# Sorting a 48-wide block for two pairs of graphs at once in a graph-network kernel

## The chip, the cores and the metric

The kernel runs on one core of a Trainium2 chip. The metric is the device time of one execution in microseconds (us), as the median of several runs. TensorE (PE) does the matrix products, VectorE (DVE) the elementwise work on whole tiles, ScalarE (ACT) activations and most copies out of PSUM, GpSimd (POOL) the indirect transfers, and SyncE (SP) starts most plain DMA transfers.

## The reference

There are 16 graphs of 1024 nodes with 64 channels, and a symmetric 0/1 adjacency of some 16 edges per node. Two layers follow one another, and each is added to its input.

```python
h = jnp.maximum(_layernorm(x, axis=-1), 0.0)
# layer 0: drop some edges of nodes with more than 10 neighbours, then
vals = jnp.where(nd[..., None], x[:, None, :, :], jnp.inf)   # nd: edges that are left
s = jnp.sort(vals, axis=2)                                   # over the neighbours
for tau, w in zip((0.25, 0.5, 0.75), (0.25, 0.5, 0.25)):     # weighted quantiles
    pos = tau * max(nv - 1, 0);  agg += w * (interpolation of s at pos)
y = relu((x + agg) @ W1 + b1) @ W2 + b2                      # times the mask
# layer 1: three graph convolutions relu(adj @ (x @ W) + b) with batch norm,
# their results side by side through one last weight, relu
```

For every node and channel, layer 0 needs three quantiles of the values of that node's live neighbours. That is where the kernel spends most of its time.

## The kernel before

**Pairs and blocks.** The graphs are handled in eight pairs, the 64 channels of two graphs on 128 partitions. In each pair the nodes are ordered by their number of live neighbours and get a place from 0 to 1023. Places with similar degrees form blocks (BLOCKS, line 39): seven blocks, 200, 192, 200, 176, 120, 72 and 48 places wide, with 11, 13, 15, 17, 19, 21 and 26 slots for neighbours, and last the tail (TAIL, line 44) of 16 places with 42 slots.

**Preparing a pair.** `prepare` (line 585) loads the adjacency rows in float32, makes an 8-bit copy `edgeT` of its transpose and stores it for later, clears the diagonal (line 686, a multiplication of 8 by 128 elements), works out which edges stay, ranks the nodes (the sign sums of line 770), scatters the rows to DRAM by place with indirect DMAs on POOL (line 778), reads them back (`lp`, line 794), transposes them, and numbers the neighbours of every place into `st.r` (line 851). At the end it rereads `h` (line 623) and splits it into three bfloat16 parts `hp`. It is a generator with 93 steps per pair.

**Gathering and sorting a block.** `gather` (line 959) builds, for several slots at a time, a one-hot tile `s` by an equality test on VectorE (line 987) and multiplies it with `hp` on TensorE (line 1018); ScalarE copies the sums to the block's tile `g` (line 1023). `sort_block` (line 1073) runs a sorting network on `g` and a spare tile `t`: each tuple of a network (NETS, line 77) is one VectorE instruction, a minimum or maximum of up to n1 by n2 rows of the block's width at once (line 935). Then the ranks that some quantile may need are multiplied by coefficients that ScalarE made (lines 868 and 871) and are added up (lines 941 and 950). The tiles `g` rotate over two buffers, `t` and `coef` have one.

**The tail** is too narrow to sort alone. In pairs 0 to 6 it is gathered into a buffer of another tag ("a", shared with the adjacency rows and the reread `h`) and sent to `tail_d` in DRAM; `sort_tails` (line 1090) reads several pairs' tails back side by side (line 1096) and sorts them together: pairs 0 to 3 at the start of pair 4, pairs 4 to 6 at the start of pair 7. The tail of pair 7 is sorted alone, at the end. POOL copies the tail's part of `st.z`, which the coefficients need, at the start of each pair's first gather (line 1065).

**Order of the work.** `weave` (line 1106) emits the network of one block instruction by instruction, and between these, by shares of the sort's cost, the gather of the next block and steps of the next pair's preparation. The shares come from SHARES (line 31): of the 93 steps, so many beside block 0, block 1 and so on, none beside block 6, where the first gather of the next pair stands. The framework's scheduler orders each engine's queue from there and keeps to this order by and large. In the last pair the second half of the computation, `later` (line 1228), takes the place of the preparation, with 7 steps beside each block (STEPS), but none beside `sort_tails`; after the last sort it goes on alone until the end.

```python
STEPS = 7
TAILS = {4: (0, 4), 7: (4, 7)}
weave(sort_block(st, n, pools), gather_block(st, n + 1, pools), steps)
```

## Time and profile before

| | |
|---|---|
| median of three runs | 3128.42 us (3122.96 to 3139.51) |
| the profiled execution: its own time | 3163.56 us |
| span from first to last instruction in it | 3161.8 us |
| PE, DVE, ACT, POOL busy | 2599.2, 2559.8, 1696.2, 619.5 us |
| mean granted TensorE clock | 0.915 |
| end of the last sort | 2832 us after the span's start |

The sum of a block's quantiles is written by the last addition of line 950, and the trace gives the start of each of these. Their distances are the stages of a pair. Of pair 2, which is one of the undisturbed ones in the middle, the seven blocks took 34.7, 40.3, 48.0, 46.5, 38.0, 46.2 and 46.8 us. In pair 7 the nine stages (block 0, tails of pairs 4 to 6, blocks 1 to 6, own tail) took 60.4, 50.5, 36.6, 78.2, 53.9, 45.6, 39.1, 39.2 and 48.7 us. What comes after the last sort takes 329.7 us.

A busy time is the time in which an engine had some instruction at work. Instructions overlap at their ends, so the mean duration of a kind of instruction, times their number, comes out above the busy time; distances between starts don't have this fault.

### The profile page before, as it was taken

The page shows a single profiled execution, that of the slowest core. Times are in us where ns is not written, and L with a number is a line of the kernel's source. Part 1 is how long each engine was busy: PE and PEld are TensorE (multiplying, and loading weights), DVE is VectorE, ACT ScalarE, POOL GpSimd, SP SyncE. Part 2 cuts the span into 40 slices and gives each one's busy share as a digit, 9 for nine tenths or more (in the row PEclk, how much of TensorE's full clock was granted, in tenths as well). Part 3 has the DMA queues.
Part 4 walks back from the last instruction along what each step waited for, and adds up shares of the span by engine and source line. Part 5 has one row for each costly group of instructions (what it writes and reads, how often), then busy time and mean ns, then how long its engine had stood idle before and what let it go on. Part 6 is the DMA issues. An engine that isn't in the chain of part 4 may idle for free.

```text
span 3161.8 us, 67201 instructions
## 1 busy us (share of the span) xinstructions
PE 2599.2 (82%) x27849; PEld 1697.4 (54%) x27849; DVE 2559.8 (81%) x5895; ACT 1696.2 (54%) x3292; POOL 619.5 (20%) x545
## 2 busy tenths in 40 slices
PE   2678978898888889885798889888986688977778
PEld 1445655565556556653565566456643456644445
DVE  4149889998999799989998999899976979963332
ACT  4764666567557755774367557745853223332221
POOL 5110161022102200330022103300422530311110
PEclk9779999999899999997899999999987799988989
DMA  4131022111211212122111211211113011122211
GB/s 138 46 104 60 3 67 70 56 55 52 66 57 54 64 56 68 46 72 47 42 64 51 66 56 57 67 56 63 48 36 75 9 41 26 49 55 54 54 54 42
DMA packets 221082, 177.45 MB, mean 56 GB/s; under 512 B 189024, under 2 KB 189152, under 8 KB 216672
## 3 DMA queue, kind: packets, MB, share of 16 engines
q1 hardware_dynamic: 141824, 125.88, 13.1%
q0 software_dynamic: 17408, 37.81, 3.9%
q10 hardware_dynamic: 61536, 9.39, 1.7%
q8 instruction: 219, 3.59, 0.5%
q14 instruction: 95, 0.78, 0.1%
HBM read 124.44 MB, written 48.55 MB: 55 GB/s over the span
## 4 chain that ended last, share of the span: by engine, by line
DVE 40%; PE 29%; ACT 12%; DMA 8%; issue 6%; another core or an unknown queue 2%; POOL 2%; ACTq 1%; DVEq 0%; POOLq 0%; SPq 0%
PE pg L1018 11%; DVE t L935 10%; DVE s L987 9%; DVE g L935 8%; PE pg L1200 5%; ACT junk L770 3%; DMA a<-in_adj 3%; DMA lp<-live_d 3%; DVE junk_v L673 2%; PE pr L845 2%; DVE g_tails L935 1%; DVE t_tails L935 1%; PE keys L763 1%; PE pf L1216 1%
## 5 line engine op out<-in xcount | busy, mean ns | idle before, releaser
L1018 PE MATMUL pg<-s,hp 128*64 128x400 bf16 (+11 forms) x16848 | 1366.5, 313 | 172.3 <-DVE s L987 138.1
L1018 PEld LDWEIGHTS <-hp 128*64 128x64 bf16 x16848 | 894.5, 112 | 553.9 <-issue 109.6
L987 DVE TENSOR_SCALAR s<-r 128x3200 bf16<-128x3200 bf16 (+25 forms) x1312 | 623.6, 521 | 103.6 <-PE pg L1018 74.9
L778 POOL DMA_INDIRECT live_d<-edge,place x128 | 261.1, 2040 | 1354.3 <-DVE place L773 1149.9
L1023 ACT COPY g<-pg 128x400 f32<-128x400 f32 (+10 forms) x384 | 169.0, 443 | 399.4 <-PE pg L1018 363.1
L935 DVE TENSOR_TENSOR t<-g 128x600 f32<-128x600 f32 (+9 forms) x524 | 315.5, 626 | 34.0 <-ACT g L1023 33.2
L1200 PE MATMUL pg<-adjT,xw 128*64 128x512 fp8e4 x2304 | 284.5, 398 | 52.8 <-ACT xw L1185 25.7
L935 DVE TENSOR_TENSOR g<-t 128x96 f32<-128x96 f32 (+16 forms) x555 | 283.2, 537 | 1.2
L1243 POOL DMA_INDIRECT agg<-agg_d,place x128 | 171.2, 1338 | 495.2 <-PE pt L1131 258.2
L671 ACT ACTIVATE edge<-a 128x1024 fp8e4<-128x1024 f32 x128 | 135.1, 1058 | 214.4 <-DMA a<-in_adj 213.9
L1200 PEld LDWEIGHTS <-xw 128*64 128x64 bf16 x2304 | 140.1, 114 | 182.4 <-issue 42.0
L868 ACT ACTIVATE coef<-z,bias 128x200 f32<-128x200 bf16 (+6 forms) x480 | 173.9, 405 | 102.3 <-DVE agg L950 66.0
L935 DVE TENSOR_TENSOR t<-t 128x192 f32<-128x192 f32 (+20 forms) x447 | 207.8, 475 | 0.2
L871 ACT ACTIVATE coef<-coef,wcol 128x200 f32<-128x200 f32 (+7 forms) x512 | 189.6, 403 | 9.3 <-issue 7.1
L673 DVE SCALAR_TENSOR_TENSOR junk_v<-a 128x1024 fp8e4<-128x1024 f32 x128 | 155.4, 1214 | 24.4 <-DMA a<-in_adj 24.4
L845 PE MATMUL pr<-liveT,upto 128*128 128x512 fp8e4 (+2 forms) x384 | 127.4, 350 | 53.1 <-ACT r L851 46.9
L770 ACT ACTIVATE junk<-keys,minus 128x1024 fp8e4<-128x1024 f32 x128 | 144.3, 1128 | 38.1 <-PE keys L763 34.3
L851 ACT CAST r<-pr 128x592 bf16<-128x592 f32 (+1 forms) x256 | 142.5, 585 | 41.1 <-PE pr L847 32.1
L794 POOL DMA_DIRECT2D lp<-live_d x128 | 89.4, 699 | 376.9 <-PE pt L809 319.3
L812 ACT ACTIVATE liveT<-pt 128x1024 fp8e4<-128x1024 f32 x128 | 130.3, 1034 | 50.5 <-PE pt L809 47.1
L752 ACT ACTIVATE edge<-q,bias 128x1024 fp8e4<-128x1024 f32 x128 | 141.8, 1108 | 22.6 <-PE q L747 22.6
L725 ACT ACTIVATE stays<-cs,back 128x1024 f16<-128x1024 f32 x128 | 136.7, 1111 | 31.1 <-PE cs L721 15.9
(182 smaller groups left out, 3879.4 us busy)
## 6 DMA issues: line engine op xcount, KB each, us to landing
a<-in_adj SPq DMA_DIRECT2D x128, 512.0 KB
adjT_d<-edgeT SPq DMA_DIRECT2D x16, 1024.0 KB
lp<-live_d POOLq DMA_DIRECT2D x128, 128.0 KB
adjT<-adjT_d SPq DMA_DIRECT2D x16, 1024.0 KB
room<-in_x SPq DMA_DIRECT2D x16, 256.0 KB
h_d<-room SPq DMA_DIRECT2D x16, 256.0 KB
h_again<-h_d SPq DMA_DIRECT2D x16, 256.0 KB
xt<-in_x SPq DMA_DIRECT2D x16, 256.0 KB
```

The source lines that it names most:

```text
L673: nc.vector.scalar_tensor_tensor(junk, a, 1.0, a, ALU.is_equal, ALU.not_equal, accum_out=odd[:, b, t : t + 1], saturate=False)
L770: nc.scalar.activation(junk, keys, AF.Sign, bias=minus[:, t : t + 1], accum_out=above[:, t : t + 1], saturate=False)
L778: sent = nc.gpsimd.indirect_dma_start(out=live_d[b][:, :], out_offset=bass.IndirectOffsetOnAxis(ap=place[:, b, t : t + 1], axis=0), in_=ed ...
L845: nc.tensor.matmul(out=pr[:, o], lhsT=upto, rhs=liveT[:, u, sl], start=True, stop=(u == 0))
L868: nc.scalar.activation(coef[:, i, :], z[:, at], AF.Abs, bias=bias(rank - (slots + 1) // 2 + tau), scale=sign)
L871: nc.scalar.activation(coef[:, i, :], coef[:, i, :], AF.Relu, bias=wcol[:, q : q + 1], scale=-w)
L935: nc.vector.tensor_tensor(view(bufs, o, n1, n2), view(bufs, a, n1, n2), view(bufs, b, n1, n2), ALU.max if op else ALU.min)
L987: nc.vector.tensor_scalar(s[:, k, :, us, w0:], r[:, :, us, at + w0 : at + W], float(LIVE + 1 + k0 + k), None, ALU.is_equal)
L1018: summed = nc.tensor.matmul(out=pg[x * C : (x + 1) * C, ks, w0:], lhsT=st.hp[:, part, x, u, :], rhs=s[:, ks, x, u, w0:], start=(whole and ...
L1023: nc.scalar.copy(g[:, k0 : k0 + n, :], pg)
L1200: nc.tensor.matmul(out=pg[cs, :], lhsT=part[:, u, cs], rhs=adjT[x][:, u, sl], start=(u == 0 and k == 0), stop=(u == NT - 1 and k == len(xw ...
L1243: nc.gpsimd.indirect_dma_start(out=agg[:, t, x, :], out_offset=None, in_=agg_d[b][:, :], in_offset=bass.IndirectOffsetOnAxis(ap=place[:, b ...
```

## The change

The block of 48 places (block 6, now named MID) is handled like the tails. In an even pair it is gathered and sent to `mid_d` in DRAM, and not sorted. In the odd pair after it, `rows_of_pairs` takes a buffer twice as wide, reads the even pair's rows back into its left half, and the odd pair's block is gathered straight into the right half; `sort_pairs` then sorts 96 places at once. An even pair has six sorting stages, an odd pair seven, and SHARES has a row for each.

In an even pair the block is gathered ahead of block 5, beside the sort of block 4, into the front of block 5's own buffer, from where it is stored; then block 5 is gathered into that buffer. The tail of an even pair is gathered in the last stage, beside the first gather of the next pair, instead of one stage ahead of that.

The tails of pairs 4 to 7 are sorted together: the tail of pair 7 is gathered first of its blocks, into the last columns of the tiles that are read back, and the tails' sort has 7 steps of `later` beside it. The parts of `st.z` for both sorts are copied by ScalarE (one copy for each pair and part) instead of POOL.

The networks of 13, 15, 19 and 26 slots are others. In instructions: 29 as before, 30 for 31, 57 for 60, and 85 for 95; the number of rows they compare is the same. The network of 13 needs 15 spare rows for 17. The multiplications by coefficients are one more for 19 and for 26 slots (the ranks stand otherwise).

The diagonal is cleared by a bitwise and of 8 by 32 words of 32 bits with a constant. Some scratch tiles are dropped or lie in others' room (the junk of the sign sums in `stays`, the junk of the bounds in PSUM, `h` of `later` in the older `hp` buffer, `step` in a pool of its own).

The diff, without the tables of the networks:

```diff
-SHARES = (10, 9, 17, 24, 20, 13, 0)
+SHARES = ((12, 12, 21, 27, 21, 0), (10, 9, 17, 24, 20, 13, 0))
 STEPS = 7
...
 
-TAILS = {4: (0, 4), 7: (4, 7)}
+TAILS = {4: (0, 4), 7: (4, 8)}
 TAIL = (1008, 1024, 21, 42)
+
+MID = len(BLOCKS) - 1
 
 
...
     nc.vector.tensor_copy(ident_16, ident)
+
+    off_diag = const.tile([P, P // 4], I32, name="off_diag")
+    nc.vector.tensor_scalar(off_diag[:, :].bitcast(U8), ident, -255.0, 255.0, ALU.mult, ALU.add)
     other_h = const.tile([P, P], BF16, name="other_h")
...
-    TW = TAIL[1] - TAIL[0]
-    tail_d = [dram.tile([P, TAIL[3], TW], F32, name=f"tail_d{p}") for p in range(NP)]
-
-    tail_z = const.tile([P, len(TAUS), NP, TW], BF16, name="tail_z")
+    MW, TW = (b[1] - b[0] for b in (BLOCKS[MID], TAIL))
+    part_d = {
+        MID: [dram.tile([P, BLOCKS[MID][3], MW], F32, name=f"mid_d{p}") for p in range(NP)],
+        MID + 1: [dram.tile([P, TAIL[3], TW], F32, name=f"tail_d{p}") for p in range(NP)],
+    }
+
+    part_z = {
+        MID: const.tile([P, len(TAUS), 2, MW], BF16, name="mid_z"),
+        MID + 1: const.tile([P, len(TAUS), 4, TW], BF16, name="tail_z"),
+    }
...
     def diagonal(e):
 
+        e = e[:, :, :].bitcast(I32)
         dims = [list(d) for d in e.ap]
-        return bass.AP(tensor=e.tensor, offset=e.offset, ap=[dims[0], [N + P, NT], [1, P]])
+        return bass.AP(tensor=e.tensor, offset=e.offset, ap=[dims[0], [(N + P) // 4, NT], [1, P // 4]])
...
         nc.sync.dma_start(out=adjT_d[b][:, :, :], in_=edgeT)
         own = diagonal(edgeT)
-        nc.vector.tensor_tensor(own, own, other_h[:, None, :].to_broadcast([P, NT, P]), ALU.mult, saturate=False)
+        nc.vector.tensor_tensor(own, own, off_diag[:, None, :].to_broadcast([P, NT, P // 4]), ALU.bitwise_and)
...
         above = work.tile([P, NT], F32, tag="above", name="above")
+
+        junk = stays[:, 0, : N // 2].bitcast(F8)
         for t in range(NT):
-            junk = work.tile([P, N], F8, tag="junk", name="junk")
             nc.scalar.activation(
                 junk, keys, AF.Sign, bias=minus[:, t : t + 1], accum_out=above[:, t : t + 1], saturate=False
             )
...
-            junk = work.tile([P, N], F8, tag="junk", name="junk")
             nc.scalar.activation(
-                junk[: 2 * NT, :], by, AF.Relu, accum_out=beyond[:, b : b + 1], saturate=False
+                by, by, AF.Relu, accum_out=beyond[:, b : b + 1], saturate=False
             )
...
-    def gather_block(st, n, pools, home=None):
+    def gather_block(st, n, pools, home=None, into=None, first=-0.2, end=0.9):
+
 
         work, ps, rows = pools
         block = (BLOCKS + (TAIL,))[n]
@@ -1060,20 +1067,23 @@
         pool, tag, bufs = home or (rows, "g", 2)
 
         def groups():
-            if n == 0:
-                for q in range(len(TAUS)):
-                    nc.gpsimd.tensor_copy(tail_z[:, q, st.p, :], st.z[:, q, TAIL[0] : TAIL[1]])
-            st.g[n] = pool.tile([P, slots, j1 - j0], F32, tag=tag, bufs=bufs, name="g")
-            send(pools, (yield from gather(st, block, st.g[n], pools)))
-            if n == len(BLOCKS) and st.p < NP - 1:
-                nc.scalar.dma_start(out=tail_d[st.p][:, :, :], in_=st.g[n])
-
-        return Steps(groups()), -(-slots // per_group(block)), -0.2, 0.9
+            if n >= MID:
+                z = part_z[n]
+                nc.scalar.copy(z[:, :, st.p % z.shape[2], :], st.z[:, :, j0:j1])
+            to = into
+            if to is None:
+                to = st.g[n] = pool.tile([P, slots, j1 - j0], F32, tag=tag, bufs=bufs, name="g")
+            send(pools, (yield from gather(st, block, to, pools)))
+            in_place = st.p % 2 if n == MID else st.p == NP - 1
+            if n >= MID and not in_place:
+                nc.scalar.dma_start(out=part_d[n][st.p][:, :, :], in_=to)
+
+        return Steps(groups()), -(-slots // per_group(block)), first, end
 
     def sort_block(st, n, pools):
 
         work, ps, rows = pools
-        block = (BLOCKS + (TAIL,))[n]
+        block = BLOCKS[n]
         j0, j1, _, slots = block
         if n == 0:
...
         yield from quantiles(work, block, (st.g[n], t), st.z[:, :, j0:j1], st.agg[:, j0:j1])
-        while st.done + P <= j1 or (j1 >= TAIL[0] and st.done < j1):
+        while st.done + P <= j1 or (n == MID - 1 and st.done < j1):
             cols = slice(st.done, min(st.done + P, j1))
             waiting.append((st.p, st.agg, cols, st.done))
             st.done = cols.stop
 
-    def sort_tails(first, end, pools):
+    def rows_of_pairs(n, first, end, sent, pools):
 
         work, ps, rows = pools
-        W = (end - first) * TW
-        g = rows.tile([P, TAIL[3], W], F32, tag="g", bufs=2, name="g_tails")
+        block = (BLOCKS + (TAIL,))[n]
+        W = block[1] - block[0]
+        g = rows.tile([P, block[3], (end - first) * W], F32, tag="g", bufs=2, name="g_pairs")
+        for p in range(first, sent):
+            nc.scalar.dma_start(out=g[:, :, (p - first) * W : (p - first + 1) * W], in_=part_d[n][p][:, :, :])
+        return g
+
+    def sort_pairs(n, first, end, g, pools):
+
+        work, ps, rows = pools
+        block = (BLOCKS + (TAIL,))[n]
+        W = block[1] - block[0]
+        whole = (end - first) * W
+        t = rows.tile([P, plan(block)[3], whole], F32, tag="t", bufs=1, name="t_pairs")
+        agg = work.tile([P, whole], F32, tag="agg_pairs", name="agg_pairs")
+        yield from quantiles(work, block, (g, t), part_z[n].rearrange("p q p2 w -> p q (p2 w)"), agg)
         for p in range(first, end):
-            nc.scalar.dma_start(out=g[:, :, (p - first) * TW : (p - first + 1) * TW], in_=tail_d[p][:, :, :])
-        yield 0.0
-        t = rows.tile([P, plan(TAIL)[3], W], F32, tag="t", bufs=1, name="t_tails")
-        agg = work.tile([P, W], F32, tag="agg_tails", name="agg_tails")
-        yield from quantiles(
-            work, TAIL, (g, t), tail_z[:, :, first:end].rearrange("p q p2 w -> p q (p2 w)"), agg
-        )
-        for p in range(first, end):
-            waiting.append((p, agg, slice((p - first) * TW, (p - first + 1) * TW), TAIL[0]))
+            waiting.append((p, agg, slice((p - first) * W, (p - first + 1) * W), block[0]))
...
-    def later(pools, done):
+    def later(pools, keep, done):
 
         one, ps = pools
+
+        old_hp = keep.tile([P, 3, 2, NT, C], BF16, tag="hp", bufs=2, name="old_hp")
 
         def first(p):
             assert p < done.sent
             xt = one.tile([P, NT, 2, C], F32, tag="xt", bufs=2, name="xt")
-            h, agg = (one.tile([P, NT, 2, C], F32, tag=k, name=k) for k in ("h", "agg"))
+            h = old_hp.rearrange("p a x t c -> p (a x t c)")[:, : 2 * N * 2 * C // P].bitcast(F32)
+            h = h.rearrange("p (t x c) -> p t x c", x=2, c=C)
+            agg = one.tile([P, NT, 2, C], F32, tag="agg", name="agg")
...
-                for n in range(last):
-                    steps = (ahead, SHARES[n], 0.0, 1.0)
+
+                paired = p % 2
+                for n in range(MID + paired):
+                    steps = (ahead, SHARES[paired][n], 0.0, 1.0)
+                    sort = sort_block(st, n, pools) if n < MID else sort_pairs(MID, p - 1, p + 1, both, pools)
                     if n == 0 and p in TAILS:
 
-                        tails = sort_tails(*TAILS[p], pools)
-                        next(tails)
-                        weave(sort_block(st, n, pools), steps)
-                        weave(tails, gather_block(st, n + 1, pools))
-                    elif n == last - 1:
+                        tails = rows_of_pairs(MID + 1, *TAILS[p], TAILS[p][1], pools)
+                        weave(sort, steps)
+                        weave(sort_pairs(MID + 1, *TAILS[p], tails, pools), gather_block(st, n + 1, pools))
+                    elif n == MID - 1 + paired:
                         ahead.rest()
                         to_come = ahead.result
-                        weave(sort_block(st, n, pools), gather_block(to_come, 0, pools))
-                    elif n == last - 2:
+                        tail = () if paired else (gather_block(st, MID + 1, pools, (early[0], "a", 2)),)
+                        weave(sort, *tail, gather_block(to_come, 0, pools))
+                    elif n == MID - 1:
+                        both = rows_of_pairs(MID, p - 1, p + 1, p, pools)
                         weave(
-                            sort_block(st, n, pools), gather_block(st, n + 1, pools),
-                            gather_block(st, last, pools, (early[0], "a", 2)), steps,
+                            sort, gather_block(st, MID, pools, into=both[:, :, MW:]),
+                            gather_block(st, MID + 1, pools, (early[0], "a", 2)), steps,
+                        )
+                    elif n == MID - 2 and not paired:
+
+                        j0, j1, _, slots = BLOCKS[n + 1]
+                        room = st.g[n + 1] = pools[2].tile([P, slots, j1 - j0], F32, tag="g", bufs=2, name="g")
+                        size = BLOCKS[MID][3] * MW
+                        mid = room.rearrange("p s w -> p (s w)")[:, :size].rearrange("p (s w) -> p s w", w=MW)
+                        weave(
+                            sort, gather_block(st, MID, pools, into=mid, end=0.35),
+                            gather_block(st, n + 1, pools, into=room, first=0.4), steps,
                         )
                     else:
-                        weave(sort_block(st, n, pools), gather_block(st, n + 1, pools), steps)
+                        weave(sort, gather_block(st, n + 1, pools), steps)
                 st = to_come
             for _ in st.number:
                 pass
@@ -1472,20 +1505,23 @@
             late = (one, inner.enter_context(tc.tile_pool(name="ps_late", bufs=2, space=PSUM)))
             done = Pair()
             done.sent = TAILS[NP - 1][0]
-            ahead = Steps(later(late, done))
-            for n in range(last + 1):
+            ahead = Steps(later(late, keep, done))
+            for n in range(MID):
                 steps = (ahead, STEPS, 0.0, 1.0)
+                sort = sort_block(st, n, pools)
                 if n == 0:
-                    tails = sort_tails(*TAILS[NP - 1], pools)
-                    next(tails)
-                    weave(sort_block(st, n, pools), steps)
-                    weave(tails, gather_block(st, n + 1, pools))
+                    tails = rows_of_pairs(MID + 1, *TAILS[NP - 1], NP - 1, pools)
+                    weave(sort, gather_block(st, MID + 1, pools, into=tails[:, :, -TW:]), steps)
+                    weave(sort_pairs(MID + 1, *TAILS[NP - 1], tails, pools), gather_block(st, n + 1, pools), steps)
                     continue
-                if n < last:
-                    weave(sort_block(st, n, pools), gather_block(st, n + 1, pools), steps)
+                if n < MID - 1:
+                    weave(sort, gather_block(st, n + 1, pools), steps)
                 else:
-                    weave(sort_block(st, n, pools), steps)
-                done.sent = NP - 1
+                    both = rows_of_pairs(MID, NP - 2, NP, NP - 1, pools)
+                    weave(sort, gather_block(st, MID, pools, into=both[:, :, MW:]), steps)
+
+                done.sent = NP - 2
+            weave(sort_pairs(MID, NP - 2, NP, both, pools), (ahead, STEPS, 0.0, 1.0))
             send(pools)
             done.sent = NP
```

## The prediction

> **What bounds the kernel now.** I read the page's busy times and its forty slices first.
>
> ```profile
> PE 2599.2 (82%) x27849; PEld 1697.4 (54%) x27849; DVE 2559.8 (81%) x5895; ACT 1696.2 (54%) x3292; POOL 619.5 (20%) x545
> ...
> PE   2678978898888889885798889888986688977778
> ...
> DVE  4149889998999799989998999899976979963332
> ```
>
> VectorE and TensorE are busy alike over the whole, but not at the same places: from slice 4 to 30, where pairs are sorted, DVE shows nines and PE eights; in the last four slices PE works almost alone. Next I cut pair 2 into its seven stages (from one final addition of line 950 to the next) and asked for the busy times. Columns: stretch, length, PE, PEld, DVE, ACT, POOL, granted clock, DMA share, GB/s.
>
> ```profile
> 844.90:879.59 34.69, 31.84 (x387) 21.27 (x385) 34.41 (x48) 19.84 (x42) 0.00 (x0) 0.96 0.14 48
> 879.59:919.88 40.29, 33.91 (x435) 23.38 (x433) 40.29 (x58) 17.92 (x35) 0.00 (x0) 1.00 0.24 82
> 919.88:967.86 47.98, 45.69 (x563) 31.62 (x560) 47.98 (x79) 29.75 (x49) 0.00 (x0) 1.00 0.15 45
> 967.86:1014.33 46.47, 38.55 (x465) 27.60 (x465) 43.90 (x85) 32.27 (x60) 21.11 (x10) 0.93 0.15 51
> 1014.33:1052.32 37.99, 36.12 (x416) 25.07 (x414) 37.30 (x97) 34.49 (x63) 7.06 (x9) 1.00 0.17 46
> 1052.32:1098.56 46.24, 38.86 (x386) 20.13 (x384) 34.24 (x134) 28.94 (x61) 12.71 (x14) 0.85 0.20 58
> 1098.56:1145.37 46.81, 38.12 (x412) 21.97 (x412) 42.28 (x126) 27.61 (x63) 3.38 (x3) 0.89 0.26 77
> ```
>
> The pair takes 300.5 us, DVE is busy for 280.4 and PE for 263.1. Blocks 0 to 4 are bound by DVE (203.9 of 207.4 us). In the stage of block 5 DVE has 12 us idle: there the chain from the scattered rows to the new `hp` ends last. The stage of block 6 is DVE again (42.3 of 46.8). PE is close behind everywhere, so DVE time saved is only worth something down to PE's own need.
>
> For the price of a sort instruction I read the timeline, by distances between starts, since durations overlap. The columns are start and duration:
>
> ```profile
> 518.35 0.24 DVE L935 TENSOR_TENSOR t<-g 128x96 f32<-128x96 f32 x1
> 518.52 0.34 DVE L935 TENSOR_TENSOR t<-t 128x192 f32<-128x192 f32 x1
> 518.79 0.24 DVE L935 TENSOR_TENSOR g<-g 128x96 f32<-128x96 f32 x1
> ```
>
> 96 elements take 0.17 us, 192 take 0.27: 1.04 ns an element and 0.07 us an instruction. The durations (0.24, 0.34) would give 0.14 us an instruction, twice too much. Last, the list of waits, SP's too (us in total, times, longest):
>
> ```profile
> PE tot L646 <- DVE edgeT L686: 30.2, 14, 7.9
> SPq L623 <- DMA tail_d<-g: 154.0, 7, 105.4
> ```
>
> PE waits about 2 us a graph for the cleared diagonal, and the load of `h_again` sits behind the store of the tail, whose buffer it takes.
>
> **What the Trainium skill says.** "Vector Engine (DVE) Microarchitecture Reference", section 5.2, gives 1.0417 ns a column plus some 75 ns an instruction after queue overlap; the trace agrees (1.04 and 70). [...]"DMA: Bandwidth & Descriptors", "Anatomy of one DMA", fits 2.0 us plus bytes over 436e3 a microsecond: for 639 KB (128 x 26 x 48 x 4 bytes) an estimate of 3.5 us. "TensorE: Matmul & The Clock Gate", Part 1, says that activity releases the throttle; the clocks above (1.00 where PE is fullest, 0.85 where it waits) agree.
>
> **The change part by part.** Counts are from the tables.
>
> Block of 48. Before, a sort was 95 comparisons, 1 product and 4 additions over 12,768 elements: 100 x 0.07 + 12,768 x 1.04 ns = 20.3 us, in each of 8 pairs 162 us. After, 85 + 2 + 4 over 25,536: 6.4 + 26.6 = 33.0, four times 132. DVE loses 30 us: an even pair 20.3 less, an odd pair 12.7 more.
>
> Tails. 194 instructions (13.6 us) and 9,296 elements a pair (9.7). Before, four, three and one pair: 52.3 + 42.7 + 23.3 = 118; after, twice four: 105. Less 13.7 us, all in pair 7.
>
> Networks of 15 and 19 slots: 1 and 2 instructions less in each pair (3 less comparisons, 1 more product), 24 x 0.07 = 1.7 us.
>
> Diagonal: an instruction now takes 1.14 us from start to start (1002.15 to 1003.29). With 256 words at the float price: 0.07 + 0.27 = 0.34. Bounds for the unseen operation: 0.2 and 1.2, so 16 graphs save between -1 and 15; I take 12.8, 1.6 a pair, part of it in PE's 30 us of waiting.
>
> Together DVE loses 58 us: 22.1 in an even pair, while an odd one gains 10.9.
>
> Even pairs (0, 2, 4, 6). DVE needs 280.4 - 22.1 = 258, PE still 263 at a clock of 0.95. PE becomes the bound: the fullest stage above has it at 45.7 of 48.0 (95%), so 263 / 0.95 = 277, and with clock won back and the `h_again` chain no longer behind the tail's store some less is possible, with imbalance more. The plan looks sound: block 6's gather and more steps go beside block 4's sort (PE 36 + about 13 = 50 us there), and no steps remain for the last stage. I take 282, a gain of 18 (range 5 to 28), and 4 x 18 = 72.
>
> Odd pairs (1, 3, 5). Their last stage has 42.3 us of DVE work and PE only 38, so the wider sort costs in full: 12.7 - 1.8 = 11 (range 6 to 15), 3 x 11 = 33. The readback is issued ahead of block 5's stage, 46 us long; the estimate of 3.5 us and the short pieces of 192 bytes are covered by it. Uncovered it would cost some 5 us each.
>
> Moved issues. In an even pair the store to `mid_d` reads a buffer that block 5's first copy overwrites: that copy, in ACT's queue, waits for the store to land, and behind it stand the copies that free PE's `pg` and the coefficients. The plan leaves 5% of the stage (2 us) for an estimate of 3.5. I count 2 us a pair, already in the 282. Four stores and four loads more are issued on ACT: `tail_d` stores took 0.33 us and `g_tails` loads 0.53 to 3.9, at most 17 us, on an engine that is busy for 54%; nothing on the path. The copies of `st.z` leave POOL (24 copies, behind them nothing that is due) for ACT: 16 at about 0.3 us, also nothing. The tail's store moves behind the `h_again` load in SP's order, a gain counted above.
>
> Pair 7. Its last two stages took 39.2 + 48.7 = 87.9 us; one sort of 33 us with the 9 us that 7 steps of `later` put on DVE (32.4 busy less 23.3 of own tail) remains: 42, say 45 with waits, so 43 less. The tails' stage (50.5 us, DVE full, PE busy for 18.4) has 9.6 us more of sorting and takes over 7 steps: 50.5 + 9.6 + 9 = 69 on DVE, beside which their PE work (35.5 in the old last stage, with 18.4 some 54) finds room: 72 with waits. Block 0's stage gets the tail's gather, some of it in its idle time: 3 more. Net 19 less (range 0 to 40). The steps that run alone after the last sort are as many as before (7 + 7 + 5 x 7 + 7 = 56 steps beside sorts, against 8 x 7 = 56), so these 329.7 us stay.
>
> The junk of the sign sums now holds `stays` longer: these are 8 activations of 1.13 us after the keys (970.66 us), and the next graph's first product that leads to a new `stays` starts at 1005.83, so the cover is 20 us.
>
> Before pair 0's sorts two diagonals stand in the open chain: 2 less.
>
> Sum: -72 + 33 - 19 - 2 = -60. The profiled execution took 3163.56 us (span 3161.8 and 1.8 around it), 1.1% above the median; 3103.6 is 0.981 of it, and 0.981 x 3128.42 = 3069 us.
>
> **The rivals.** (a) PE is the bound almost at once: DVE's saving only turns into DVE idle time, an even pair gains 6 and pair 7 gains 5: -24 + 33 - 5 - 2 = 2, about 3130. For it: PE 263 of 300. Against: PE's 95% in a full stage. (b) The chain matters more than busy times: an even pair loses most of a stage (46.8 us, less what moves) and gains 28, pair 7 gains 35: -112 + 33 - 35 - 2 = -116, factor 0.963, 3014 us. For it: 12 us of DVE idle in block 5's stage. (c) Slower: the stage of block 4 in even pairs carries two gathers through one buffer; ACT stands until the store has landed, PE runs out of its three `pg` buffers, and the steps of `find_live` behind it, which must now end a stage earlier, delay the first gather of the next pair. At 20 us in each even pair the gain of 18 turns into a loss of 2: 8 + 33 - 19 - 2 = 20 more, 3148 us. It decides from 15 us a pair on (the total is then zero). For it: the exact order in that buffer; against: the store is an estimate of 3.5 us. That the change doesn't do what it says is hardly a rival: counts and widths are in the tables, only the price of the bitwise operation is open.
>
> **How the numbers follow.** Forecast 0.50, (a) 0.17, (b) 0.18, (c) 0.15. A measurement here tells about 0.5% (16 us) from no change. Faster by more: forecast and (b), 0.68; same: (a), 0.17; slower: (c), 0.15. The forecast's own range, the ends of its terms not all on one side, is 3035 to 3105. The overall range reaches past both (a) and (b): 3005 to 3142; it leaves out (c) and what lies beyond (b), some 0.2.
>
> **What would show it.** Stages of even pairs: six, their sum near 282 us with PE at 93% or more; odd pairs near 311, all of the growth in the last stage; line 686's successor at about 0.4 us; pair 7's last sort ending some 60 us sooner than 2832, with 330 us behind it. Wrong would be: a long wait of ACT for the store of `mid_d`, even pairs above 297, or odd pairs that don't grow.

## The result and the profile after

The changed kernel takes 3140.4 us (median of 20 runs, 3130.3 to 3156.6), the kernel before on the same chip 3128.3 (20 runs, 3112.0 to 3141.5). The ratio is 1.0042, 95% interval 1.0024 to 1.0061. The forecast was 3069. The profiled execution took 3133.3 us with a span of 3131.5. That of the kernel before (3163.6 us) is not one of these 20 runs.

VectorE did lose its work. From the page of the changed kernel:

```profile
PE 2567.9 (82%) x27831; PEld 1722.4 (55%) x27857; DVE 2504.5 (80%) x5242; ACT 1683.3 (54%) x3212; POOL 488.5 (16%) x521
...
PE   2678998987889889875798898789986689878778
...
DVE  4049889998998799989998999899886878873332
```

DVE has 55.3 us less than before (forecast 58), and 653 instructions fewer. But where pair 7 is sorted (slices 29 to 35) its digits are now sixes to eights, where the kernel before has nines too. Pair 2, cut into its stages as before (stretch, length, PE, PEld, DVE, ACT, POOL, clock, DMA share, GB/s):

```profile
835.30:867.80 32.50, 26.28 (x324) 18.09 (x322) 32.50 (x44) 16.57 (x37) 0.00 (x0) 0.95 0.11 36
867.80:908.00 40.20, 37.48 (x447) 24.34 (x444) 39.91 (x67) 20.70 (x38) 0.00 (x0) 0.95 0.24 82
908.00:957.40 49.40, 45.40 (x523) 32.21 (x523) 49.08 (x72) 33.28 (x59) 0.00 (x0) 0.97 0.18 55
957.40:1004.20 46.80, 45.32 (x550) 31.24 (x547) 43.75 (x85) 36.02 (x62) 12.57 (x10) 1.00 0.16 55
1004.20:1066.30 62.10, 47.75 (x570) 30.65 (x572) 43.20 (x116) 42.65 (x76) 27.10 (x22) 0.92 0.24 70
1066.30:1122.60 56.30, 50.53 (x603) 36.47 (x601) 51.87 (x139) 33.28 (x76) 0.00 (x0) 0.94 0.29 82
```

Six stages, 287.3 us, DVE 260.3 (forecast 258). In the fifth stage nobody is full: 62.1 us with PE at 47.8 and DVE at 43.2. (The same stage took 51.7, 53.0 and 49.7 us in pairs 0, 4 and 6.)

The diagonal, from DVE's timeline (start, duration): the next instruction starts 0.34 us later, as forecast.

```profile
973.52 0.41 DVE L692 TENSOR_TENSOR edgeT<-edgeT,off_diag 128x256 int32<-128x256 int32 x1
973.86 0.88 DVE L941 TENSOR_TENSOR t<-t,g 128x704 f32<-128x704 f32 x1
```

In the list of waits PE still waits for the cleared diagonal, 7 us less than before, and VectorE waits 90.8 us for gathers in the second half, line 1158:

```profile
DVE agg L1158 <- DMA agg<-agg_d,place: 90.8, 8, 15.0
...
PE tot L652 <- DVE edgeT L692: 23.5, 10, 7.3
```

The trace ahead of the change shows 22.6 us of that wait, in two pieces. But that is no measure of the change: a second trace of the same kernel, b_again below, has

```profile
DVE agg L1142 <- DMA agg<-agg_d,place: 84.4, 8, 15.8
```

and the changed kernel on that chip has 90.4. Whatever the kernel, traces from two of the chips have 70 to 92 us here while steps of the second half run beside the sorts, those from three others 22 to 53, so such waits can only be compared on one chip.

The even pairs take 523.5 (pair 0, from the start of the span), 287.3, 334.1 and 270.8 us, where they took 544.8, 300.5, 351.9 and 296.3; the odd ones 311.8, 308.0 and 306.4 for 300.1, 292.5 and 293.9; pair 7 470.8 for 452.1; the rest 318.8 for 329.7. In this pair of executions the even pairs gain 77.8, the odd ones lose 39.7, pair 7 loses 18.7, the rest gains 10.9: 30.3 us less. Yet the medians differ by 12 the other way. The profiled execution of the kernel before was 35 us above the median of its runs, that of the changed kernel 7 below: two traces from single executions cannot decide over half a per cent.

### The profile page after: what moved, and what is told of

Its sections match the earlier page's. It is cut to its first block, busy times and chain, and to the rows that moved or that the text cites. A ratio compares the mean times of both kernels' runs of the same rounds, so it can differ in the third digit from the quotient of the medians.

```text
span 3131.5 us, 66495 instructions
## 1 busy us (share of the span) xinstructions
PE 2567.9 (82%) x27831; PEld 1722.4 (55%) x27857; DVE 2504.5 (80%) x5242; ACT 1683.3 (54%) x3212; POOL 488.5 (16%) x521
## 5 line engine op out<-in xcount | busy, mean ns | idle before, releaser
L1024 PE MATMUL pg<-s,hp 128*64 128x400 bf16 (+12 forms) x16848 | 1362.5, 313 | 132.7 <-DVE s L993 124.4
L1029 ACT COPY g<-pg 128x400 f32<-128x400 f32 (+8 forms) x366 | 159.9, 440 | 351.8 <-PE pg L1024 344.4
L941 DVE TENSOR_TENSOR t<-g 128x800 f32<-128x800 f32 (+20 forms) x416 | 297.1, 736 | 15.3 <-ACT g L1029 14.3
L941 DVE TENSOR_TENSOR g<-t 128x800 f32<-128x800 f32 (+5 forms) x392 | 265.6, 706 | 0.9
L874 ACT ACTIVATE coef<-z,bias 128x200 f32<-128x200 bf16 (+4 forms) x392 | 149.7, 422 | 91.2 <-DVE agg L956 60.1
L877 ACT ACTIVATE coef<-coef,wcol 128x200 f32<-128x200 f32 (+6 forms) x460 | 173.3, 411 | 2.1 <-issue 1.4
L941 DVE TENSOR_TENSOR t<-t 128x600 f32<-128x600 f32 (+18 forms) x272 | 169.9, 634 | 0.4
L731 ACT ACTIVATE stays<-cs,back 128x1024 f16<-128x1024 f32 x128 | 136.6, 1111 | 37.2 <-DVE look L712 20.8
L777 ACT ACTIVATE stays<-keys,minus 128x1024 fp8e4<-128x1024 f32 x128 | 144.1, 1126 | 23.3 <-PE keys L769 22.5
L816 PE MATMUL pt<-ident_h,lp 128*128 128x128 bf16 x1024 | 86.1, 234 | 82.1 <-DMA lp<-live_d 61.8
L684 PE MATMUL ptE<-ident_h,edge 128*128 128x128 bf16 x1024 | 86.5, 234 | 75.9 <-ACT edge L677 54.1
```

The source lines that it names most:

```text
L777: nc.scalar.activation(junk, keys, AF.Sign, bias=minus[:, t : t + 1], accum_out=above[:, t : t + 1], saturate=False)
L874: nc.scalar.activation(coef[:, i, :], z[:, at], AF.Abs, bias=bias(rank - (slots + 1) // 2 + tau), scale=sign)
L877: nc.scalar.activation(coef[:, i, :], coef[:, i, :], AF.Relu, bias=wcol[:, q : q + 1], scale=-w)
L941: nc.vector.tensor_tensor(view(bufs, o, n1, n2), view(bufs, a, n1, n2), view(bufs, b, n1, n2), ALU.max if op else ALU.min)
L1024: summed = nc.tensor.matmul(out=pg[x * C : (x + 1) * C, ks, w0:], lhsT=st.hp[:, part, x, u, :], rhs=s[:, ks, x, u, w0:], start=(whole and ...
L1029: nc.scalar.copy(g[:, k0 : k0 + n, :], pg)
```

## The experiments

All timed runs of one group were made on one chip, beside the kernel before; levels differ by 1.8% between chips (kernel before: 3128 to 3186 us). Besides the ratio the table gives, from one trace each, the end of pair 6, and pair 7 with the rest. Single traces scatter: a_again and a_nosteps have the same queues up to pair 7 and ran on one chip, and pair 6 ends 6 us apart; the traced executions of a_third and bs_lpsp2 were 18 and 16 us faster than the median of their runs, that of a_again 13 slower.

| group | kernel | ratio, 95% | end of pair 6 | pair 7 and rest |
|---|---|---|---|---|
| 0 | before | | 2380.0 | 781.8 |
| 0 | changed | 1.0042 (1.0024 to 1.0061) | 2341.9 | 789.6 |
| 1 | b_again | 0.9993 (0.9980 to 1.0007) | 2371.6 | 784.3 |
| 1 | a_again | 0.9989 (0.9974 to 1.0004) | 2364.6 | 796.6 |
| 1 | b_small | 1.0062 (1.0037 to 1.0086) | 2394.1 | 777.3 |
| 1 | a_nosteps | 1.0037 (1.0022 to 1.0052) | 2358.4 | 805.8 |
| 2 | a_lpsp | 1.0062 (1.0038 to 1.0087) | 2384.4 | 803.3 |
| 2 | b_lpsp | 1.0330 (1.0305 to 1.0356) | 2486.1 | 784.6 |
| 2 | bs_lpsp | 1.0215 (1.0185 to 1.0246) | 2453.4 | 781.5 |
| 2 | a_ahead | 0.9907 (0.9883 to 0.9930) | 2341.1 | 792.1 |
| 3 | a_third | 1.0074 (1.0051 to 1.0096) | 2336.8 | 789.7 |
| 3 | a_lpsp2 | 0.9891 (0.9856 to 0.9927) | 2298.2 | 794.0 |
| 3 | b_lpsp2 | 0.9886 (0.9860 to 0.9912) | 2318.3 | 768.1 |
| 3 | a_even | 1.0064 (1.0046 to 1.0082) | 2349.9 | 790.6 |
| 4 | bs_lpsp2 | 0.9910 (0.9877 to 0.9942) | 2348.0 | 776.5 |
| 4 | a_best | 0.9987 (0.9970 to 1.0003) | 2361.8 | 805.1 |
| 4 | a_s0 | one run | 2343.3 | 900.4 |
| 4 | b_s0 | one run | 2366.0 | 887.2 |
| 5 | a_eight | 0.9854 (0.9831 to 0.9876) | 2329.6 | 811.6 |
| 5 | b_ref | 0.9915 (0.9895 to 0.9935) | 2372.1 | 793.6 |

**Group 1: both kernels again, the small edits alone, the tails' stage without steps.** b_again and a_again are unedited. b_small is the kernel before with the new networks and

```diff
+        e = e[:, :, :].bitcast(I32)
-        nc.vector.tensor_tensor(own, own, other_h[...], ALU.mult, saturate=False)
+        nc.vector.tensor_tensor(own, own, off_diag[...], ALU.bitwise_and)
```

a_nosteps is the changed kernel with

```diff
-weave(sort_pairs(MID + 1, ...), gather_block(st, n + 1, pools), steps)
+weave(sort_pairs(MID + 1, ...), gather_block(st, n + 1, pools))
```

> The kernel before, unchanged, with a second profile. Its first profile (3163.6 us) lies 35 us above its median (3128), that of the changed kernel 7 us below its own. Theory 1: pairs 1 and 2 again take about 300 us each and the last sort ends near 2832 us; then the loop of pairs did gain about 39 us and the last pair lost it. Theory 2: that first profile was a slow execution; the spans of the pairs are some 3 to 5 us shorter (last sort near 2800), and the loop gained little.

> The changed kernel, unchanged, with a second profile on the chip of the others. Both theories: 3140 us, last sort near 2815 us, even pairs 271 to 287, odd pairs 306 to 312, pair 7 about 470.

> The kernel before with only the other networks and the bitwise diagonal. 10 instructions less in each sort of the 48-wide block (8 x 9 x 0.07 = 5 us), 1.7 us of the other networks, 12.8 us of the diagonal: 20 us less on VectorE, so some 3110 us if VectorE is the bound (forecast's view); 3128 if TensorE is (rival a); more than 3128 if the order that the scheduler makes of it is worse.

> The changed kernel without the 7 steps of the second half beside the sort of the tails; these steps follow after the last sort. If the tails' stage is long (92.5 us instead of 72) because VectorE stands before line 1158's addition until the rows are gathered, the stage falls to about 62 us and the end grows by at most 36: 3135 to 3145 us, so a draw. If the early steps have a cost beyond their own time (they push the later ones against gathers that have just been issued), it is faster, 3120 or less. If the steps are well placed there, slower by 20 us or more.

The change is worth nothing on this chip either. In the two traces the even pairs gain 48.9 us and the odd ones lose 42.1. Less work alone, b_small, is slower by 0.6%, though it takes work off VectorE and adds none. Its loss lies in pairs 0 to 6 (2394.1 for 2371.6), in block 5's stage (47 to 52 us for 40 to 44 in most pairs). POOL's timeline there and PE's (start, duration, idle time before in brackets) show what PE waits for:

```profile
1045.09 0.54 POOL L790 DMA_DIRECT2D lp<-live_d  x1 [1.47 <-PE pt L805]
1045.93 1.04 POOL L774 DMA_INDIRECT live_d<-edge,place  x1 [0.31 <-issue]
...
1060.31 1.29 POOL L774 DMA_INDIRECT live_d<-edge,place  x1 [0.30 <-issue]
1061.61 1.15 POOL L790 DMA_DIRECT2D lp<-live_d  x2
```

```profile
1064.01 1.89 PE L805 MATMUL pt<-ident_h,lp 128*128 128x128 bf16 x16 [10.89 <-DMA lp<-live_d]
```

Two of the first graph's readbacks `lp` now stand behind the second graph's eight scatters. PE's queue waits 10.9 us for them, and gathers wait behind. In the kernel before, POOL's queue has that order in the preparations of pairs 1 and 5 only, in b_small in all seven beside sorts (with one or two readbacks), in the changed kernel in those of pairs 2, 4 and 6, which run in the odd pairs. The diff moves no line of it: with other instructions around it, the framework's scheduler chose another order. The order alone doesn't fix the stage's length: in b_again the two preparations that have it take 42.7 and 48.6 us in that stage, the others 36.7 to 43.7.

The same queue lies behind the long fifth stage of the even pairs. POOL, PE and DVE in the changed kernel's pair 2:

```profile
1027.47 1.22 POOL L785 DMA_INDIRECT live_d<-edge,place  x1 [0.30 <-issue]
1029.00 11.79 POOL L785 DMA_INDIRECT live_d<-edge,place  x1 [0.30 <-ACT coef L874]
1041.09 0.96 POOL L785 DMA_INDIRECT live_d<-edge,place  x1 [0.30 <-issue]
```

```profile
1047.72 1.03 PE L816 MATMUL pt<-ident_h,lp 128*128 128x128 bf16 x8 [9.14 <-DMA lp<-live_d]
```

```profile
1049.37 1.91 DVE L993 TENSOR_SCALAR s<-r 128x1008 bf16<-128x1008 bf16 x5 [9.42 <-PE pg L1024]
```

One scatter of some 1 us takes 11.8 while VectorE works without a pause (1025.2 to 1040.0, until 1037.8 almost only on the sort); then PE waits 9.1 us for the readback and VectorE 9.4 for PE. The scatter ends 0.84 us after VectorE's last instruction, and that is no accident. In the 20 traces here 126 scatters took over 5 us. In 91 of them VectorE paused before the scatter's end, often for 0.03 us only, and every one of these ended 0.83 to 0.91 us after the first pause; in the other 35 it never paused. So a scatter that is held up gets through at VectorE's first pause, if not before. What holds it is argued, not shown: no run took the sort away from beside a scatter, and 891 scatters of under 1.5 us ran beside a VectorE without a pause too. The Trainium skill, "SBUF — State Buffer", section "Who interferes with whom", says that a VectorE instruction with two SBUF inputs, as the sort's are, contends with a GpSimd one that reads SBUF, and that descriptor generation on GpSimd can be starved by VectorE. That fits, if the scatter reads its places so; but the page also says that its own probe did not see such two-input instructions stall a DMA. Where such a scatter fell on the first graph (12 to 20 us in the kernel before), little was lost: in pair 2, fourth stretch of the prediction's table, VectorE is idle for 2.6 us.

a_nosteps: pair 7 falls from 477.4 to 435.4 and the rest grows from 319.2 to 370.4. Seven steps cost 42 us beside sorts and 51 alone, so they gain 9 by the traces (16 by the medians). The prediction had counted 9 us for them in the tails' stage.

**Group 2: the readback on another queue, and the gather of the second half earlier.** In a_lpsp, b_lpsp and bs_lpsp (from the changed kernel, the kernel before and b_small):

```diff
-load = nc.gpsimd.dma_start(out=lp, in_=live_d[b][t * P : (t + 1) * P, :])
+load = nc.sync.dma_start(out=lp, in_=live_d[b][t * P : (t + 1) * P, :])
```

In a_ahead, from the changed kernel:

```diff
+turn = 0
 while now.step():
     yield
-    if ahead is not None and ahead.step():
+    if ahead is not None and (turn == 0 or turn > 3) and ahead.step():
         yield
+    turn += 1
```

> The changed kernel with one line different: the readback of the scattered rows (lp, line 801) is issued on SP instead of POOL. Theory Q: what the change lost lies in POOL's queue. There the second graph's scatter (8 indirect DMAs) stands behind the readbacks of the first graph, and in pairs 1, 3, 5 of the changed kernel the last two readbacks of the first graph stand behind the second graph's scatter; block 5's stage took 52 to 55 us there, 41 to 46 before. In pairs 0, 2, 4 the late scatter falls beside a sort and takes 11 to 12 us for one instruction, and that stage takes 62 us, 50 in pair 6, where it doesn't happen. With the readback on SP the scatter follows as soon as the places are known: three times 12 and three times 8 to 10 us less, 40 to 65 in all, ratio to the kernel before 0.980 to 0.988. Rival R: these stages are long because PE has as much work as they are long, at its clock; the queue of the readback is no matter, and the ratio stays at 0.999 to 1.004.

> The kernel before with the same one line on SP. Theory Q: before, only the preparations in pairs 0 and 4 have two readbacks of the first graph behind the second graph's scatter; two stages lose 5 us less and POOL's 12-us scatters in other pairs are slack, so 5 to 15 us less, ratio 0.995 to 0.999. Rival R: no difference, 1.000. If it gains as much as the changed kernel does, the line is an improvement of its own and not the place where the change's gain went.

> The kernel before with only the new networks and the bitwise diagonal (1.006 of the kernel before in an earlier run, though VectorE has some 15 us less to do), and the readback on SP. Theory Q: its loss came from the order in POOL's queue, where each of the seven preparations beside sorts has one or two readbacks of the first graph behind the second graph's scatter (block 5's stage 47 to 51 us, 40 to 44 before). With the readback on SP it loses that: about 7 times 5 = 35 us less than 1.006, ratio 0.992 to 0.997, a few us below the kernel before with the same line. Rival R (the new instructions themselves cost more, or the clock is lower): it stays near 1.006.

> The changed kernel; in `later` the loads and the 16-row gather of the next pair are still issued beside the first step of the present one, but its remaining steps start only from the fifth step on, the number of steps being the same. Theory L: pair 7 lost its forecast gain to the chain of `later`, where VectorE stands in front of the addition that waits for POOL's gather (90.8 us in 8 waits in the changed kernel, 22.6 in 2 before). With the gather four steps ahead these waits fall below 30 us and pair 7 with the rest (796 us) loses 10 to 30 us, ratio 0.990 to 0.996. Rival M: the waits only stand in for others, as PE's and ACT's steps are the chain; the sum stays at 790 to 800 and the ratio at 0.999 to 1.004.

All three with the readback on SP missed. Block 5's stage was as short as theory Q had it (41 to 46 us in the odd pairs of a_lpsp), but that doesn't speak for theory Q: a_ahead, on the same chip with the readbacks still in POOL's queue, has 44.5 to 45.6. Block 3's stage grew to 60 to 66. In b_lpsp's list of waits:

```profile
DVE edgeT L686 <- DMA adjT_d<-edgeT: 116.1, 9, 16.3
```

The store of `adjT_d`, issued on SP too, now stood behind waiting readbacks, and VectorE, in front of the diagonal, waited for it. The expectations had left out what else SP issues.

a_ahead did to the wait what was wanted:

```profile
DVE agg L1158 <- DMA agg<-agg_d,place: 22.7, 2, 12.6
```

On the same chip a_lpsp, whose pair 7 has the steps as they were, waits 52.9 us there, and pair 7 and the rest take 803.3 us for 792.1 in a_ahead. That is 11 us less, as theory L would have it; yet on other chips the unedited kernel takes 789.6 to 796.6, as rival M would. No unedited one ran beside a_ahead, so the run doesn't decide between the two. Nor does its ratio of 0.991, since up to pair 7 all its queues are those of the changed kernel.

**Group 3: both moves together, and other shares.** a_lpsp2 and b_lpsp2 add to the readback on SP

```diff
-nc.sync.dma_start(out=adjT_d[b][:, :, :], in_=edgeT)
+nc.scalar.dma_start(out=adjT_d[b][:, :, :].bitcast(F32), in_=edgeT[:, :, :].bitcast(F32))
```

a_even is the changed kernel with

```diff
-SHARES = ((12, 12, 21, 27, 21, 0), ...
+SHARES = ((13, 14, 23, 29, 14, 0), ...
```

> The changed kernel once more, unedited, as the common reference of this call: the two earlier comparisons gave 1.0042 and 0.9989, so a version of it must be compared on the same chip. Expected 0.993 to 1.005, with stages of about 62 us where a scatter of 9 to 12 us falls on the second graph of pairs 0, 2 or 4, and about 50 where none does.

> The changed kernel with the readback of the scattered rows on SP, as before, and now the store of the 8-bit adjacency (line 690) on ACT. With the readback alone moved, the kernel was 1.006: the odd pairs' block-5 stage fell from 52 to 55 us to 41 to 46, as theory Q said, but the store of adjT_d stood behind the waiting readbacks in SP's queue, and VectorE waited for it in front of the diagonal (54.9 us, 5 times; block 3's stage 61 to 66 us for 47 to 49). With the store on ACT, behind the copy that makes its data, theory Q expects that stage back at 47 to 50 and block 5's at 41 to 46: three odd pairs of 300 us instead of 308, ratio 0.985 to 0.995. Rival R: other waits take their place and it stays within 0.004 of the unedited kernel of this call.

> The kernel before with the same two lines. The readback alone on SP made it 1.033, with block 3's stage at 61 to 63 us for 45 in every pair (VectorE waited 116 us in 9 times for the store of adjT_d). Theory Q: with the store on ACT it comes back to 0.993 to 1.000, since only pairs 0 and 4 have anything to win from the readback. If it gains as much as the changed kernel, the pair of lines is an improvement of its own.

> The changed kernel with the even row of SHARES at 13, 14, 23, 29, 14, 0 instead of 12, 12, 21, 27, 21, 0: the preparation runs 7 steps ahead of its old place when block 4's sort begins. Theory S: block 4's stage of pairs 0, 2 and 4 (62 us, PE busy 48, DVE 43) is long because the second graph's scatter falls beside a sort without gaps, takes 10 to 12 us, and PE and DVE then wait for its readback. With the scatter in block 3's stage the wait is covered; block 4's stage falls to 48 to 52, the first three stages grow by 3 to 6 in all, three pairs gain 6 to 10: ratio 0.990 to 0.997 of the unedited kernel of this call. Rival T: the stages before are full of PE work (44 to 45 of 47 to 49 us), so the steps that move there cost what the stall gives back: within 0.003 of the unedited one, or slower.

a_third, unedited, came out above the range given for it. Against it the two lines take 1.8% off the changed kernel (0.9891 for 1.0074), and they take 1.1% off the kernel before, more than theory Q gave it. So the place of these transfers in the queues cost both kernels, the changed one more; but it wasn't all, since they end level. No run moved the store alone; VectorE waits 8.0 us for it in all in the changed kernel's trace, little beside the 52 us that were gained. Where the kernel before gains is not shown: block 5's stage took 42 us on average in b_again and takes 38 in b_lpsp2, but 43 and 44 in the same code on two other chips (b_s0 and b_ref). In the changed kernel that stage falls from 50 to 55 us in the odd pairs of a_third to 37 to 39. Odd pairs now take 300.2, 294.7 and 295.4, with the growth where it was forecast, in the last stage (57.7 to 59.3 for 45.4 to 48.0). Two executions of the same stage in a_lpsp2, pairs 2 and 4, with the same queues, differ by one scatter of 11.7 us:

```profile
997.30:1048.20 50.90, 45.89 (x578) 29.66 (x578) 43.20 (x116) 42.65 (x77) 8.75 (x8) 1.00 0.28 85
1620.60:1682.20 61.60, 47.68 (x579) 30.95 (x580) 43.56 (x116) 42.88 (x77) 18.63 (x8) 0.92 0.24 70
```

POOL is busy 9.9 us longer and the stage is 10.7 us longer; PE has 1.8 us more, at a clock of 0.92 for 1.00, and DVE and ACT no more than 0.4. a_even got rid of the long scatters in even pairs but not of the stage (61 to 67 us): there the readbacks stood behind the scatter again.

**Group 4: small edits and shares once more, and pair 7 without the second half.** bs_lpsp2 is b_small with the two lines, a_best is a_lpsp2 with a_even's shares; a_s0 and b_s0 are a_lpsp2 and b_lpsp2 with

```diff
-STEPS = 7
+STEPS = 0
```

> The kernel before with the new networks, the bitwise diagonal, the readback on SP and the store of adjT_d on ACT. Theory Q: the small edits (1.006 of the kernel before by themselves) lost their gain only because they turned the order in POOL's queue, where readbacks of the first graph then stood behind the second graph's scatter in all pairs. Without readbacks in that queue, VectorE's 15 to 20 us less show: 0.981 to 0.986 of the kernel before, where the two lines alone gave 0.9886. Rival R: the small edits cost by themselves, and it is at 0.990 or above.

> The changed kernel with readback on SP, store of adjT_d on ACT (0.9891 of the kernel before), and the even row of SHARES at 13, 14, 23, 29, 14, 0. With the two lines, block 4's stage still took 60 and 61 us in pairs 0 and 4, where a scatter of 12 us falls on the second graph, and 51 and 46 in pairs 2 and 6, where it doesn't. With the readback in POOL's queue the other shares left that stage at 61 to 67 us: no scatter took over 5 us in it any more, but the last two readbacks of the first graph stood behind it. With both mended theory Q expects 48 to 52 in all four even pairs: 20 us less, ratio 0.980 to 0.986. Rival T: the stage is as long as PE's work in it plus the chain from places to numbers, and stays at 60; 0.988 to 0.992.

> The changed kernel with the two lines, and no steps of the second half beside the sorts of pair 7 (STEPS = 0; all of them run after the last sort). Together with the same edit of the kernel before it shows the bare sorts of pair 7. Theory L: without steps the merged sorts take about what their VectorE work is: 360 us before and 350 to 360 after (VectorE's need is 1 us less, two stage ends fewer), and pair 7's loss of 27 us between the two kernels with steps comes from what steps cost beside the longer tails' sort and the last one. Rival V: the stages lose by their own gathers (the tails' stage 72, the last one 45), and after is 15 us or more longer without steps too.

> The kernel before with the two lines, and no steps of the second half beside the sorts of pair 7. Expected: pair 7 at about 360 us for 446 with steps, so that 56 steps cost some 85 us beside sorts; after the last sort some 300 us more than 322.

The ratio of bs_lpsp2 missed, but chips differ here: b_lpsp2 has 0.9886 on one and 0.9915 on another. Up to pair 6, b_s0 has b_lpsp2's code and ran on the same chip: 2348.0 for 2366.0. There the small edits gain 18 us, where with readbacks in POOL's queue they lost 22.5. The sign is theory Q's, but bs_lpsp2's trace was 16 us below its median and b_s0 is a single run, so only the end of the loss can be relied on, not the gain. a_best refutes theory Q for the shares: no scatter over 5 us is left in its even pairs, and block 4's stage still takes 54 to 64 us. More PE work lies in it, 53.3 us in pair 2 for 49.9 in a_s0, whose stage is as long (58.9) with a scatter of 9.7:

```profile
1014.30:1073.10 58.80, 53.27 (x629) 32.88 (x628) 45.91 (x120) 43.35 (x79) 8.59 (x8) 0.97 0.28 81
```

Up to pair 6 it is 18.5 us longer than a_s0, a single run, which has the old shares.

Pair 7 without steps, a_s0 and then b_s0, as one stretch each:

```profile
2343.30:2675.70 332.40, 188.91 (x1994) 123.79 (x1988) 306.28 (x720) 85.49 (x248) 43.20 (x32) 0.78 0.12 22
```

```profile
2366.00:2699.70 333.70, 198.41 (x2050) 128.92 (x2052) 306.79 (x928) 89.86 (x278) 34.47 (x32) 0.78 0.11 21
```

The bare sorts are 1.3 us apart, and VectorE's work in them 0.5; both take less than the 350 to 360 us that were expected. With steps pair 7 takes 472.9 and 445.7 (group 3, another chip): 56 steps cost some 140 us in the changed kernel and 112 before, or 128 with b_ref's pair 7 of 461.7 on a third chip. The second half alone took 568.0 and 553.5 us here; in a_s0 PE waited once, 27.9 us, for its first addition, which b_s0's waits don't show; that would cover these 14.5 us.

**Group 5: steps placed as before.** a_eight is a_lpsp2 with the edit of a_nosteps and `STEPS = 8`; b_ref is b_lpsp2 unedited.

> The changed kernel with the readback on SP and the store of adjT_d on ACT, and in pair 7 no steps of the second half beside the tails' sort but 8 instead of 7 beside each of the seven other sorts: 56 steps as before, placed as the kernel before has them. With 7 steps everywhere pair 7 took 472.9 us and the rest 321.1 (kernel before, same two lines: 445.7 and 322.4), though the bare sorts take 332.4 and 333.7. Theory P: the 28 us come from the place: steps beside the tails' sort (194 short instructions) wait most and push the one-hot products back. Then pair 7 falls to 445 to 455 and the rest stays at 320 to 325: ratio to the kernel before 0.982 to 0.986. Rival N: it is the number of sorts to spread over (eight instead of nine, the last only one) that counts: eight steps in a stage cost more than seven, and pair 7 stays at 465 to 480, ratio 0.988 to 0.992.

> The kernel before with the same two lines once more (0.9886 on another chip), beside the run above on the same chip: 0.986 to 0.992. It says whether any version of the change is faster than the kernel before when both have the two lines: under theory P the version above is 0.3 to 0.6% faster, under rival N it is the same within 0.3%.

Pair 7 stays at 480.2 us (461.7 in b_ref), as rival N had it, though the ratio fell in theory P's range. The tails' stage falls to 74.4, but the stage two blocks on takes 82.4 and the last 72.9. Still a_eight is the fastest version on its chip, 0.9854 for 0.9915, since pairs 0 to 6 gain 42.5 us over b_ref; so the change, with its queues mended, is worth some 0.6% there. On group 3's chip, with 7 steps beside every sort (a_lpsp2 and b_lpsp2), it was worth nothing.

## Why the prediction was wrong

**What held.** VectorE's prices: 55.3 us less for 58, 260.3 in an even pair for 258, the diagonal 0.34 us for 0.34. Even pairs gain and odd pairs lose in every comparison. No wait for the store of `mid_d`, rival (c)'s place, is in the list of waits. (The fit behind the estimate of 3.5 us for this store is given for transfers that GpSimd issues, and this one is issued on ACT; the trace shows no landing for it.) On SP, the load of `h_again` no longer waits for the tail's store (154 us before):

```profile
SPq L628 <- DMA agg_d<-o: 56.3, 2, 55.6
```

In its place loads of the adjacency rows, which share that buffer, now wait 40.7 us for the store.

The parts of the sum, from the traces of each group (us, minus is a gain; pair 0 counts from the start of the span, and group 0's two traces need not come from one chip):

| part | forecast | group 0 | group 1 | a_lpsp2 for b_lpsp2 | a_eight for b_ref |
|---|---|---|---|---|---|
| even pairs and start | -74 | -77.8 | -48.9 | -40.8 | -59.5 |
| odd pairs | 33 | 39.7 | 42.1 | 20.8 | 17.1 |
| pair 7 | -19 | 18.7 | 16.4 | 27.2 | 18.5 |
| rest | 0 | -10.9 | -4.2 | -1.3 | -0.5 |

**The step that failed: pair 7, "net 19 less (range 0 to 40)".** It lost 16 to 27 us in every comparison with all 56 steps. VectorE's work was not misjudged. Both wider sorts are in the stage sums, and they leave it 1 us less to do there (0.5 in the bare sorts of a_s0 and b_s0). The other 18 us were idle time and a gather that was to run in idle time, and the idle time did not go. Here is pair 7 as one stretch, b_again and then a_again, on one chip:

```profile
2371.60:2832.60 461.00, 355.89 (x3350) 238.71 (x3350) 374.01 (x1026) 139.94 (x362) 143.10 (x80) 0.86 0.19 43
2364.60:2842.00 477.40, 372.89 (x3396) 254.69 (x3394) 374.80 (x820) 140.51 (x337) 96.84 (x80) 0.85 0.19 42
```

VectorE is busy for the same 374 us, and idle for 102.6 instead of 87.0. The prediction put its gain on the last two stages and took the idle time there as saved; that idle time belongs to the chain of the second half, which goes where its steps go. Here are the changed kernel's tails' stage and last stage:

```profile
2402.00:2494.50 92.50, 62.24 (x561) 45.18 (x559) 77.97 (x231) 24.48 (x62) 16.71 (x16) 0.83 0.07 13
...
2752.80:2812.80 60.00, 42.32 (x332) 27.29 (x330) 44.35 (x111) 16.54 (x39) 22.98 (x16) 0.91 0.26 70
```

and the kernel before's tails' stage and its last two:

```profile
2440.40:2490.90 50.50, 18.37 (x183) 13.79 (x179) 50.50 (x207) 12.74 (x44) 36.94 (x15) 0.69 0.10 22
...
2744.30:2783.50 39.20, 36.28 (x317) 22.54 (x314) 38.24 (x162) 16.45 (x44) 4.08 (x4) 0.96 0.11 19
2783.50:2832.20 48.70, 35.50 (x252) 21.39 (x246) 32.36 (x206) 15.71 (x49) 11.66 (x13) 0.82 0.27 76
```

The tails' stage grew by 42 us, not 21: DVE has 27.5 more to do (forecast 18.6) and stands for 14.5. The last stage takes 60, not 45, with DVE idle for 15.6. Steps priced at 1.3 us of VectorE each, the waits taken as hidden, cost 6 (a_nosteps: 42 for 7). With +19 in place of −19 the sum would have been −22, and the forecast 3107 us.

**The second failure: the even pairs' size and its certainty.** The -77.8 of group 0 looks like the forecast, but by luck: it leans on the trace of the kernel before that stood 35 us above the median. Compared on one chip the even pairs gain 41 to 60 us, not 74. Pairs 0 to 6 together were to gain 41; they gain 7.0 in group 1 and, with the two lines in both kernels, 20.1, 22.7 and 42.5 (groups 3, 4 and 5). The prediction looked for rival (c) in ACT's queue and for SP's `h_again`, but not in POOL's, though it named that queue only for the copies that leave it. There the steps of `find_live`, which were to run a stage earlier, met a queue whose order the scheduler sets anew. Rival (c)'s number, 3148, came nearest and block 4's stage in even pairs is where it looked, but the store that it blames held nothing up, and the even pairs gained. PE reached 88% of pair 2, not 93, and the even pairs gained 10 us or more on average, not 6, so rival (a) is not why either.

**The third: the scale.** The kernel before was read from one execution, 35 us above its median, and its excess was spread in proportion (0.981). Block 5's stage, which depends on POOL, took 46.2 us in the pair that was cut, and 40.3 in the same pair of b_again; so some 6 of the 18 us that this pair was to gain were that execution's. The clocks in that table were read too simply as well: PE is busy for 84% both in block 1's stage, at a clock of 1.00, and in block 5's, at 0.85.

**What stays open.** Why 56 steps cost some 12 to 28 us more beside eight sorts than beside nine is not settled: their place (a_eight) is not the cause, and the late gather (a_ahead) was not tested against an unedited kernel on its chip. Nor is it why the gain of pairs 0 to 6 differs between chips by a factor of two.

## What to carry to other kernels

Split every forecast gain into work that goes and idle time that is to go: here VectorE's work in pair 7 fell by 1 us, and the other 18 were idle time and did not come. Before costing a rearrangement, list what every DMA queue holds around it, in order, since one queue of small transfers with two graphs in it can come out in another order without a line of it being edited. And idle time that a latency chain leaves does not vanish with the stage it was seen in.

## What the runs showed of the hardware

Of 2560 single indirect scatters on POOL in the 20 traces most took 1 to 2 us, and 126 took 5 to 20.2 us beside a busy VectorE, some in every kernel; those that saw VectorE pause ended 0.83 to 0.91 us after its first pause, even one of 0.03 us. Readbacks of 128 KB landed 2.3 us after their issue from POOL (median in the changed kernel, 5.5 at most), so where PE waits 9 to 11 us for one, it is what stands ahead of it in POOL's queue, not the transfer, that makes it late. The same kernel differed by up to 1.8% between chips, and the changed kernel's ratio was 1.0042, 0.9989 and 1.0074 on three of them: for a change of half a per cent the versions to be compared have to share a chip, and so have their lists of waits.
